# A sparse attention layer: ring of 17 in place of 20 gather slots, and a later write of the flag for the branch

## The chip, the cores and the metric

The kernel runs on one core of a Trainium2 chip. The metric is the device time of one execution in microseconds. Before the change, five runs gave a median of 1885.34 us, between 1882.17 and 1888.16 us. One more execution was taken with the hardware profiler; all durations come from it.

The engines have short names in the profile: PE (TensorE, matmuls and transposes), PEld (its weight loads), DVE (VectorE), ACT (ScalarE), POOL (GpSimd) and SP (SyncE). Each works through its own queue in order.

## The reference

One graph layer over 4096 nodes with 512 features, 8 heads of 64, and a 4096 x 4096 adjacency matrix of 0 and 1 with some 17 edges in a row:

```python
hs, ht = layer_norm(x), layer_norm(h_target)             # ln1
q = (ht @ Wq + bq) / 8;  k = hs @ Wk + bk;  v = hs @ Wv + bv
logits = where(edge_mask != 0, q @ k.T, -1e30)           # for each head
ctx = softmax(logits) @ v
ht = layer_norm(ht + ctx @ Wo + bo)                      # ln2
x = layernorm(x + ht + gelu(ht @ W1) @ W2)               # W1: 512 x 2048
```

## The kernel before

The kernel uses that the matrix is sparse. It has two programs in one: a fast path for inputs like these, and `general_path`, a dense version that a branch at the end runs only when the fast path has found that its assumptions fail (a row with too many neighbours, a mask that is not all ones, sums out of range). The branch reads one number, `flag`.

**Lists (to about 650 us).** For each tile of 128 rows of the matrix, four quarters of 1024 columns are loaded. ACT takes the sign of a quarter (L727), DVE multiplies it by the column's number and takes the eight largest of each segment (L734). The numbers of a row's neighbours end in a record of that row. `sort` ranks the rows of one half of the matrix by their number of neighbours (`PARTS`: the first part is rows 0 to 2047, the second 2048 to 4095), and scatters the records in that order to DRAM (L852). So a tile of 128 targets later has a fixed capacity, from 39 down to 11 neighbours (`CAPS_A`, `CAPS_B`). Meanwhile PE projects all nodes to keys and values and writes them as rows of 4 KB to DRAM, `kvd`.

**Attention (about 305 to 1770 us).** A tile's neighbours are taken in groups of up to three (`S`, list `SG`: 211 groups, 603 gathers). For each neighbour POOL issues one indirect DMA (L962, called from `issue`) that brings 128 rows of 4 KB, 512 KB, into one slot of the `ring`. Per group DVE multiplies the keys by the query (L1189), sums per head (L1193), ACT takes the exponential (L1197, L1207; a third neighbour's values are scaled on ACT, L1170 and L1173), DVE multiplies the values by it (L1153) and, in the second part, adds the second neighbour's values to the first's (L1157). PE transposes the slots into one PSUM sum (L1161). A slot is free when L1161, or for the second neighbour of the second part L1157, has read it. `finish` divides, applies `Wo` (L1074 to L1088) and the second layer norm; its power on POOL is L686. The query of a tile comes from `front`: a gather of target rows, a scale on ACT (L988), transposes (L992) and `Wq` (L1001, L1003).

**Feed-forward (about 330 to 1866 us).** Pairs of tiles (`GROUPS`, 17 of them, the first and last single) go through W1, GELU (L1297, L1300) and W2 (L1306) in `feed`. `end` adds, normalises (L1253 to L1270; power again L686) and scatters the rows to the output by an indirect DMA (L1274).

**What sets the order.** The stages are Python generators that yield a cost; `_weave` always continues the one that is furthest behind, so attention, feed-forward and list work are interleaved as the program is written. The framework then places the instructions in the engines' queues by its own estimate of the times, and adds the waits. In the attention stage each pair of tiles has the same cost (`UNIT`), whatever its number of neighbours.

**The ring.** It has 20 slots of 4 KB a partition. While the first part is processed, groups use slots 0 to 16. Slots 17 and 18 (`wide`) and 19 (`tools`) are the work space of the lists of the second part: quarters of the matrix, their signs, and the small tiles of `sort`. From group 106 on, the first whose tile belongs to the second part by its place (`i >= NA`), groups use all 20 slots. `request(k)`, called when the values of the group before k have been handed on (line after `values` in `attention`), issues the gathers of all groups up to k + 4 in the first part and k + 5 in the second (`AHEAD` is 4).

**The verdict and the branch.** `verdict` collects what was found wrong into one number in PSUM (L1242), and DVE writes `flag` from it (L1243). It stands at the end of `attention`. After all work, `values_load` (L1421) makes each of the five engines load `flag` into a register, and `tc.If` (L1422) is a branch on each of them.

Of the kernel before, what the change touches and what calls it, by code (L numbers as in the profile page):

```python
# [17 lines left out]
P = 128  # L18
# [349 lines left out]
U8 = mybir.dt.uint8  # L368
# [75 lines left out]
def adj_resnorm_kernel(  # L444
# [58 lines left out]
    S = 3  # L503


    RING = (17, 20)

# [8 lines left out]

    flag = const.tile([1, 1], I32, name="flag")

    def row_bcast(pool, v, name):
# [12 lines left out]
    with tc.tile_pool(name="keep", bufs=1) as keep:  # L532
# [17 lines left out]
        with ExitStack() as late:  # L550
# [13 lines left out]

            ring = kp.tile([P, RING[1], 2 * D], F32, name="kv")
            wide = [ring[:, 17 + i, :].bitcast(I32) for i in range(2)]
            tools = ring[:, 19, :]
            signs = [tools[:, i * QW // 4:(i + 1) * QW // 4].bitcast(U8) for i in range(3)]
            dec_w = tools[:, 768:768 + SEG * 8].bitcast(U16).rearrange("p (b s e) -> p b s e",
                                                                       b=2, s=SEG)  # L570
            turns = {"wide": 0, "signs": 0}

            def turn_of(name, places):
                turns[name] += 1
                return places[turns[name] % len(places)]

# [31 lines left out]
            def list_constants():  # L608
                io = turn_of("wide", wide)
# [4 lines left out]
                io = turn_of("wide", wide)  # L614
# [92 lines left out]
            def quarter(i, h):  # L707
                if i < NA + FILL:
                    a = ring[:, (i * NQ + h) % DEEP, :].bitcast(I32)
                else:  # L710
                    a = turn_of("wide", wide)
                nc.sync.dma_start(a, adj[i * P:(i + 1) * P, h * QW:(h + 1) * QW])
                return a

            def edges(i):
# [4 lines left out]
                for h in range(NQ):  # L720
# [4 lines left out]

                    sg = turn_of("signs", signs)
                    nc.scalar.activation(sg, a, AF.Sign, accum_out=dpart[:, i, h:h + 1])  # L727
# [11 lines left out]
                    yield 2.0  # L739
                dec = dec_w  # L740
                nc.vector.tensor_single_scalar(dec[:, 0], cand, 255, op=ALU.bitwise_and)
# [64 lines left out]
            def sort(part):  # L806
# [5 lines left out]
                nc.vector.tensor_copy(R[:, :, DEG], deg[:, me])  # L812
                dif, rank = tools[:, 928:928 + n], tools[:, 944:944 + n]
                ranki, b16 = tools[:, 960:960 + n].bitcast(I32), tools[:, 976:984].bitcast(BF16)
# [3 lines left out]
                nc.vector.tensor_scalar(dif, deg[:, me], 0.0, float(NB - 1), op0=ALU.max,  # L818
                                        op1=ALU.min)
                nc.vector.tensor_scalar(b16, dif, -1.0, float(NB - 1), op0=ALU.mult, op1=ALU.add)  # L820
                if part:
                    oh = turn_of("wide", wide).bitcast(BF16)
                else:
                    oh = wp.tile([P, NB * n], BF16, name="oh")
# [3 lines left out]
                ohf = oh.rearrange("p b i -> p (b i)")  # L828
                pos = turn_of("wide", wide).bitcast(F32)
                pos = pos[:, :NB * n].rearrange("p (b i) -> p b i", b=NB)  # L830
# [11 lines left out]
                for c in range(2):  # L842
# [3 lines left out]
                    nc.vector.tensor_add(posf[:, sl], pa, posf[:, sl])  # L846
                nc.vector.tensor_mul(pos, pos, oh)
                nc.vector.tensor_reduce(rank, pos.rearrange("p b i -> p i b"), AX.X, ALU.add)
                nc.vector.tensor_copy(ranki, rank)
                yield 10.0  # L850
# [160 lines left out]
            place = [0]  # L1011
            for i, _, n in SG:
                if place[-1] + n > RING[i >= NA]:
                    place[-1] = 0
                place.append(place[-1] + n)
            first_b = next(k for k, (i, _, _) in enumerate(SG) if i >= NA)
            issued = [0]

# [4 lines left out]

            def request(k):


                ahead = AHEAD + (1 if k >= first_b else 0)
                while issued[0] <= min(k + ahead, len(SG) - 1):
                    issue(issued[0])
                    mine = set(range(place[issued[0]], place[issued[0]] + SG[issued[0]][2]))  # L1030
                    for m in range(k, issued[0]):
                        assert not mine & set(range(place[m], place[m] + SG[m][2]))
                    issued[0] += 1

            def issue(k):

                i, j0, n = SG[k]
                if j0 == 0:
# [97 lines left out]
            def attention():  # L1136
# [37 lines left out]

                request(0)
                yield 0.0
                k = 0
                for group in GROUPS:
# [3 lines left out]
                    for i in group:  # L1182
                        cps = ps.tile([P, KC, P], F32, name="cps", bufs=2)
                        while k < len(SG) and SG[k][0] == i:
# [15 lines left out]
                            if pend:  # L1200
                                values(*pend.pop())
                                request(k)
                            advance()
# [17 lines left out]
            def verdict():  # L1221
# [20 lines left out]
                nc.tensor.matmul(pb, b1, ones_bf[:, 0:1], start=True, stop=True)  # L1242
                nc.vector.tensor_scalar(flag, pb, 0.5, None, op0=ALU.is_gt)  # L1243

# [37 lines left out]
            def feed(g):  # L1282
# [88 lines left out]
            def prepare():  # L1371
# [10 lines left out]
                nm = turn_of("wide", wide)  # L1382
                nc.sync.dma_start(nm[:NT, :P], nodemask.rearrange("(c p) -> c p", p=P))
# [71 lines left out]
```

## Time and profile before

| what | value |
|---|---|
| median of five runs | 1885.34 us |
| profiled execution, its own time | 1887.54 us |
| its span, first to last instruction | 1885.5 us |
| PE busy | 1701.6 us, 7030 matmuls |
| DVE busy | 1429.2 us |
| ACT busy | 1233.3 us |
| POOL busy | 885.0 us |
| gathers (L962, kv) | 603, 1136 ns each on POOL |
| last matmul ends | 1866.8 us |
| granted PE clock, mean | 0.957 |

The page gives busy time by engine, then the costliest groups of instructions by line, then waits. A line such as `DVE a L10 <- PE b L20: 5.0, 3, 2.1` in the view of waits says that VectorE stood idle before the instructions of line 10 that write a, for 5.0 us in 3 waits, the longest 2.1 us, until PE's instruction of line 20 released it. "issue" in place of a releaser is idle time for which the profile shows no wait. The table by stages has for each stretch of time its length, and then each engine's busy time with its number of instructions, the granted PE clock, the DMA engines' busy share and GB/s. A row of one line's instructions gives their number, minimum, median and maximum duration in ns, and the first and last start.

### The profile page before, as it was taken

The numbers are of one execution on the slowest core, as the hardware profiler recorded it, in microseconds if no ns is written. First come the engines' busy times: TensorE is split into PE (matmuls) and PEld (weight loads), VectorE is DVE, ScalarE is ACT, GpSimd is POOL, SyncE is SP. The second block draws the span as 40 slices with busy tenths as digits, with TensorE's granted clock in tenths as the row PEclk, the third lists the DMA queues.
The fourth block names the chain that finished last, engine by engine and source line by source line (L and its number), as shares of the span: only waits on it lengthen the run. The fifth ranks groups of instructions, "written<-read, shape, count | busy, mean of one in ns | idle before, by whom it ended". The sixth has DMA issues, their size and how long they took to land. (4 is left out here: it accounts for less than half of the span.)

```text
span 1885.5 us, 22906 instructions
## 1 busy us (share of the span) xinstructions
PE 1701.6 (90%) x7030; PEld 1101.8 (58%) x7030; DVE 1429.2 (76%) x2595; ACT 1233.3 (65%) x3127; POOL 885.0 (47%) x804
## 2 busy tenths in 40 slices
PE   7989883698998989999989989999989899999996
PEld 3444331565665656676666666666656565666664
DVE  6999855999998747777868889888777778778200
ACT  5777634586886747776777777876757567677311
POOL 1000144644545565657576676665646554644101
PEclk9999987798999989999999999999999999999998
DMA  9999949878876656868688788777756666765000
GB/s 352 372 371 372 354 155 351 315 273 299 315 276 227 206 179 217 279 216 294 232 283 293 259 283 299 273 238 236 245 194 215 230 224 216 244 215 180 23 1 24
DMA packets 147757, 463.28 MB, mean 246 GB/s; under 512 B 24468, under 2 KB 29160, under 8 KB 147624
## 3 DMA queue, kind: packets, MB, share of 16 engines
q0 software_dynamic: 95696, 342.19, 53.2%
q1 hardware_dynamic: 44112, 96.44, 14.3%
q10 hardware_dynamic: 7816, 23.08, 3.2%
q8 instruction: 58, 0.95, 0.2%
q14 instruction: 75, 0.61, 0.1%
HBM read 430.76 MB, written 30.89 MB: 245 GB/s over the span
## 5 line engine op out<-in xcount | busy, mean ns | idle before, releaser
L962 POOL DMA_INDIRECT kv<-kvd,rec x603 | 685.1, 1136 | 484.9 <-PE cps L1161 214.8
L1297 PE MATMUL pf<-h2T,w 128*128 128x256 f32 (+1 forms) x2176 | 481.0, 373 | 5.6 <-issue 2.8
L1306 PE MATMUL po<-w,gt 128*128 128x512 f32 x1024 | 464.3, 594 | 0.0
L1297 PEld LDWEIGHTS pf<-h2T,w 128*128 128x128 f32 x2176 | 393.8, 194 | 68.3 <-issue 20.0
L1189 DVE TENSOR_TENSOR kv<-kv,tq 128x1536 f32<-128x1536 f32 (+2 forms) x211 | 352.4, 1676 | 106.7 <-DMA kv<-kvd,rec 83.3
L1173 ACT ACTIVATE kv<-kv,pa 128x64 f32<-128x64 f32 x1520 | 391.6, 336 | 3.8
L1193 DVE TENSOR_REDUCE lg<-kv 128x24 f32<-128x1536 f32 (+2 forms) x211 | 350.5, 1667 | 1.5 <-ACT pa L1170 0.3
L1161 PE MATMUL cps<-ident,kv 128*128 128x128 f32 x2008 | 266.8, 281 | 45.9 <-DMA kv<-kvd,rec 23.7
L1161 PEld LDWEIGHTS cps<-ident,kv 128*128 128x128 f32 x2008 | 240.1, 145 | 116.5 <-issue 89.2
L1306 PEld LDWEIGHTS po<-w,gt 128*128 128x128 f32 x1024 | 186.3, 191 | 188.5 <-issue 188.0
L1153 DVE TENSOR_TENSOR kv<-kv,p 128x1024 f32<-128x1024 f32 (+1 forms) x211 | 249.6, 1189 | 50.9 <-ACT p L1197 40.9
L686 POOL TENSOR_TENSOR n_rs<-n_ve,mhalf 128x2 f32<-128x2 f32 (+2 forms) x51 | 45.2, 887 | 343.7 <-DVE n_ve L679 171.2
L727 ACT ACTIVATE kv<-kv 128x1024 uint8<-128x1024 int32 x128 | 134.9, 1055 | 84.8 <-DMA kv<-in_adj_dram 46.7
L927 PE MATMUL pq<-wk,h2T 128*128 128x512 f32 x256 | 125.8, 636 | 15.9 <-ACT h2T L912 9.4
L1300 ACT ACT_TABLE_LOAD x107 | 137.3, 1283 | 1.6
L734 DVE MAX8 cand<-kv 128x8 uint16<-128x103 uint16 (+1 forms) x640 | 132.1, 252 | 0.5
L1300 ACT ACTIVATE gt<-pf 128x512 f32<-128x512 f32 x128 | 76.4, 597 | 85.0 <-PE pf L1297 72.3
L1001 PE MATMUL t<-wq,tq 128*128 128x512 f32 x256 | 117.5, 601 | 13.7 <-ACT tq L995 9.8
L1088 PE MATMUL t<-wo,rb 128*128 128x512 f32 x256 | 119.7, 612 | 1.7 <-DVE rb L1078 1.7
L927 PE MATMUL pq<-wv,h2T 128*128 128x512 f32 x256 | 115.5, 593 | 0.4 <-ACT tq L929 0.4
L1197 ACT ACTIVATE p<-lg 128x24 f32<-128x24 f32 (+2 forms) x179 | 33.6, 188 | 107.2 <-DVE lg L1193 77.8
L927 PEld LDWEIGHTS pq<-wk,h2T 128*128 128x128 f32 x256 | 50.7, 205 | 83.2 <-issue 60.4
(155 smaller groups left out, 1561.5 us busy)
## 6 DMA issues: line engine op xcount, KB each, us to landing
kv<-in_adj_dram SPq DMA_DIRECT2D x128, 512.0 KB
kvd<-tq ACTq DMA_DIRECT2D x24, 512.0 KB
kv<-kvd,rec POOLq DMA_INDIRECT x603
kv<-in_L_gnn_h_target_dram SPq DMA_DIRECT2D x32, 256.0 KB
kv<-in_x_dram SPq DMA_DIRECT2D x15, 512.0 KB
rest_d<-gid SPq DMA_DIRECT2D x32, 160.0 KB
w<-in_L_gnn_W_dram SPq DMA_DIRECT2D x4, 1024.0 KB
kvd<-kv ACTq DMA_DIRECT2D x8, 512.0 KB
```

The costliest lines, as they stand in the source:

```text
L727: nc.scalar.activation(sg, a, AF.Sign, accum_out=dpart[:, i, h:h + 1])
L734: nc.vector.max(cand[:, h * SQ + s, :], wd[:, w0:w1])
L927: nc.tensor.matmul(pkv, hT[:, kc, j * P:(j + 1) * P], w[:, kc, :], start=kc == 0, stop=kc == KC - 1)
L962: nc.gpsimd.indirect_dma_start(out=dst, out_offset=None, in_=table[:, :], in_offset=bass.IndirectOffsetOnAxis(ap=idx, axis=0))
L1153: nc.vector.tensor_tensor(v4, v4, p[:, j0:j0 + m, :].unsqueeze(3) .to_broadcast([P, m, H, HD]), ALU.mult)
L1161: nc.tensor.matmul(cps[:, c, :], kv[:, j, D + c * P:D + (c + 1) * P], ident, is_transpose=True, start=j0 + j == 0 and c == 0, stop=j0 + n ...
L1173: nc.scalar.mul(v, v, pa[:, hd:hd + 1])
L1189: nc.vector.tensor_tensor(kv[:, :n, :D], kv[:, :n, :D], tq[:, :D].unsqueeze(1).to_broadcast([P, n, D]), ALU.mult)
L1193: nc.vector.tensor_reduce(lg[:, :n, :], kv[:, :n, :D].rearrange("p j (h d) -> p j h d", h=H), AX.X, ALU.add)
L1297: nc.tensor.matmul(pf[:, k, :], w1[(f0 + k) // KC][:, kc, (f0 + k) % KC * P:((f0 + k) % KC + 1) * P], h2T[:, kc, :w], start=kc == 0, stop= ...
L1300: nc.scalar.activation(gt, pf, AF.Gelu_apprx_tanh)
L1306: nc.tensor.matmul(po[j], gt[:, k, j * P:(j + 1) * P], w2[(f0 + k) // KC][:, (f0 + k) % KC, :], start=False, stop=f0 + k == FC - 1, skip_g ...
```

## The change

The change takes the ring back to one depth and one distance of requests, gives the lists' work space tiles of its own, and puts one instruction between the verdict and the flag.

- `RING` is 17 for both parts. `wide`, `tools`, `signs` and `turn_of` go; quarters, signs, and the tiles of `sort` and of the list's decoding are tiles of the pool `lp` with the same sizes and numbers of buffers.
- `request` goes. `attention` first issues groups 0 to 4, and then `issue(k + AHEAD)` for each group, in both parts. `issue` itself is the same.
- `verdict` writes `raised`. In `feed`, after the last `end` has been emptied, DVE computes `flag` as the maximum of `raised` and `raised`, with one element of the last result row, `xs[-1]`, as a scalar operand that is bypassed. So this instruction waits for the last activation (L1270), and each engine's load of `flag` waits for this instruction.

```diff
-    RING = (17, 20)
+    RING = 17
...
     flag = const.tile([1, 1], I32, name="flag")
+    raised = const.tile([1, 1], F32, name="raised")
...
-            ring = kp.tile([P, RING[1], 2 * D], F32, name="kv")
-            wide = [ring[:, 17 + i, :].bitcast(I32) for i in range(2)]
-            tools = ring[:, 19, :]
-            signs = [tools[:, i * QW // 4:(i + 1) * QW // 4].bitcast(U8) for i in range(3)]
...
+            ring = kp.tile([P, RING, 2 * D], F32, name="kv")
...
                 else:
-                    a = turn_of("wide", wide)
+                    a = lp.tile([P, QW], I32, name="a", bufs=2)
                 nc.sync.dma_start(a, adj[i * P:(i + 1) * P, h * QW:(h + 1) * QW])
...
-                    sg = turn_of("signs", signs)
+                    sg = lp.tile([P, QW], U8, name="sg", bufs=3)
...
-            for i, _, n in SG:
-                if place[-1] + n > RING[i >= NA]:
+            for _, _, n in SG:
+                if place[-1] + n > RING:
                     place[-1] = 0
                 place.append(place[-1] + n)
-            first_b = next(k for k, (i, _, _) in enumerate(SG) if i >= NA)
-            issued = [0]
...
-            def request(k):
-                ahead = AHEAD + (1 if k >= first_b else 0)
-                while issued[0] <= min(k + ahead, len(SG) - 1):
-                    issue(issued[0])
...
-                    issued[0] += 1
...
-                request(0)
+                for k in range(AHEAD + 1):
+                    issue(k)
...
                                 values(*pend.pop())
-                                request(k)
+                                issue(k + AHEAD)
...
-                nc.vector.tensor_scalar(flag, pb, 0.5, None, op0=ALU.is_gt)
+                nc.vector.tensor_scalar(raised, pb, 0.5, None, op0=ALU.is_gt)
...
                     while ends:
                         wind_up()
+                    nc.vector.scalar_tensor_tensor(flag, raised, xs[-1][0:1, 0:1], raised,
+                                                   op0=ALU.bypass, op1=ALU.max)
```

More of the change, by code (lines that the diff above doesn't have):

```diff
@@ L561, in adj_resnorm_kernel @@
             psi = mid.enter_context(tc.tile_pool(name="psi", bufs=1, space=PSUM))
-            ring = kp.tile([P, RING[1], 2 * D], F32, name="kv")
-            wide = [ring[:, 17 + i, :].bitcast(I32) for i in range(2)]
-            tools = ring[:, 19, :]
-            signs = [tools[:, i * QW // 4:(i + 1) * QW // 4].bitcast(U8) for i in range(3)]
[L569 to L575, printed above, removed]
+            ring = kp.tile([P, RING, 2 * D], F32, name="kv")
             def xrows(n):
@@ L608, in list_constants @@
             def list_constants():
-                io = turn_of("wide", wide)
+                io = lp.tile([P, QW], I32, name="a", bufs=2)
                 nc.gpsimd.iota(io[:, :SQ * WS], pattern=[[0, SQ], [2, WS]], base=1,
@@ L613, in list_constants @@
                 nc.vector.tensor_copy(lio, io[:, :WQ])
-                io = turn_of("wide", wide)
+                io = lp.tile([P, QW], I32, name="a", bufs=2)
                 nc.gpsimd.iota(io[:, :2 * SEG], pattern=[[1, 2], [QW, NQ], [2 * WS, SQ]], base=0,
@@ L739, in edges @@
                     yield 2.0
-                dec = dec_w
+                dec = lp.tile([P, 2, SEG, 8], U16, name="dec")
                 nc.vector.tensor_single_scalar(dec[:, 0], cand, 255, op=ALU.bitwise_and)
@@ L812, in sort @@
                 nc.vector.tensor_copy(R[:, :, DEG], deg[:, me])
-                dif, rank = tools[:, 928:928 + n], tools[:, 944:944 + n]
-                ranki, b16 = tools[:, 960:960 + n].bitcast(I32), tools[:, 976:984].bitcast(BF16)
+                dif = pool.tile([P, n], F32, name="dif")
                 nc.vector.scalar_tensor_tensor(dif, deg[:, me], float(RE), cnt[:, me], op0=ALU.min,
@@ L819, in sort @@
                                         op1=ALU.min)
+                b16 = pool.tile([P, n], BF16, name="b16")
                 nc.vector.tensor_scalar(b16, dif, -1.0, float(NB - 1), op0=ALU.mult, op1=ALU.add)
                 if part:
-                    oh = turn_of("wide", wide).bitcast(BF16)
+                    oh = pool.tile([P, QW], I32, name="a", bufs=2).bitcast(BF16)
                 else:
@@ L828, in sort @@
                 ohf = oh.rearrange("p b i -> p (b i)")
-                pos = turn_of("wide", wide).bitcast(F32)
+                pos = pool.tile([P, QW], I32, name="a", bufs=2).bitcast(F32)
                 pos = pos[:, :NB * n].rearrange("p (b i) -> p b i", b=NB)
@@ L847, in sort @@
                 nc.vector.tensor_mul(pos, pos, oh)
+                rank = pool.tile([P, n], F32, name="rank")
                 nc.vector.tensor_reduce(rank, pos.rearrange("p b i -> p i b"), AX.X, ALU.add)
+                ranki = pool.tile([P, n], I32, name="ranki")
                 nc.vector.tensor_copy(ranki, rank)
@@ L1022, in step @@
                     del gens[i]
-            def request(k):
-                ahead = AHEAD + (1 if k >= first_b else 0)
-                while issued[0] <= min(k + ahead, len(SG) - 1):
-                    issue(issued[0])
-                    mine = set(range(place[issued[0]], place[issued[0]] + SG[issued[0]][2]))
-                    for m in range(k, issued[0]):
-                        assert not mine & set(range(place[m], place[m] + SG[m][2]))
-                    issued[0] += 1
             def issue(k):
+                if k >= len(SG):
+                    return
                 i, j0, n = SG[k]
@@ L1381, in prepare @@
                     nc.vector.tensor_copy(Rf[:, :, RST + 1], nm[:, i0:i0 + n])
-                nm = turn_of("wide", wide)
+                nm = lp.tile([P, QW], I32, name="a", bufs=2)
                 nc.sync.dma_start(nm[:NT, :P], nodemask.rearrange("(c p) -> c p", p=P))
```

## The prediction

> **What bounds the kernel now.** I read the page's busy shares first, then the busy time by stage, then the waits of VectorE and GpSimd in each stage, then the instructions at the branch.
>
> ```profile
> span 1885.5 us, 22906 instructions
> PE   1701.6 (90%) x7030; PEld 1101.8 (58%) x7030; DVE 1429.2 (76%) x2595; ACT 1233.3 (65%) x3127; POOL 885.0 (47%) x804
> ```
>
> TensorE (PE) is busy 90% of the span and takes its work in one fixed order, so the time is PE's work plus PE's idle time. What matters is which late result leaves PE idle. The stages below are cut at 1024 us, where the requests for the second part begin, at 1250 us, where the second part's first two pairs of tiles are done, and at 1740 us, where the last gathered rows are used.
>
> ```profile
> core 0: us, PE busy (x) PEld busy (x) DVE busy (x) ACT busy (x) POOL busy (x), PEclk, DMA share, GB/s
> 700.00:1024.00 324.00, 312.13 (x1476) 218.01 (x1475) 251.62 (x253) 236.67 (x645) 197.02 (x177) 1.00 0.76 257
> 1024.00:1250.00 226.00, 211.49 (x922) 143.28 (x921) 207.41 (x215) 175.17 (x486) 150.76 (x131) 0.98 0.80 277
> 1250.00:1740.00 490.00, 458.60 (x1918) 305.37 (x1916) 377.12 (x401) 336.58 (x883) 265.44 (x232) 0.98 0.66 222
> 1740.00:1871.00 131.00, 126.80 (x540) 84.67 (x537) 20.30 (x82) 31.02 (x65) 10.32 (x13) 1.00 0.05 15
> ```
>
> The first row is the first part's attention, which already runs with a ring of 17 and requests four groups ahead: PE is idle 11.9 of 324 us (3.7%). The next two rows run with 20 slots and five groups ahead: PE is idle 14.5 of 226 us and 31.4 of 490 us (6.4% each). In the row from 1024 us VectorE (DVE) is busy 207.4 of 226 us (92%): this is the one stage where DVE has little room. From 1740 us PE does feed-forward alone.
>
> Waits of DVE in the three attention stages, one line from 700 to 1024 us, two from 1024 to 1250 us and one from 1250 to 1740 us:
>
> ```profile
> DVE kv L1189 <- DMA kv<-kvd,rec: 29.0, 15, 5.2
> ...
> DVE kv L1153 <- ACT p L1197: 6.6, 9, 2.3
> DVE kv L1189 <- issue: 4.8, 2, 2.6
> ...
> DVE kv L1189 <- DMA kv<-kvd,rec: 24.3, 12, 6.8
> ```
>
> L1189 is the first use of a gathered group. With four groups ahead it waits 29.0 us in 324 us for the gathers; with five ahead it waits for none in the stage from 1024 us. What GpSimd (POOL) waits for between 1024 and 1760 us, before it issues gathers:
>
> ```profile
> POOL kv L962 <- DVE kv L1157: 74.0, 36, 6.1
> POOL kv L962 <- PE cps L1161: 68.7, 35, 5.9
> ```
>
> L1157 and L1161 are the last readers of a slot. So the gathers are issued when a slot comes free: the ring's depth sets the lead.
>
> **The change part by part.** *The lists' work space* goes from three ring slots (12 KB a partition) to tiles of the same sizes and counts. In the order of the two programs every engine has the same instructions up to the first request of the second part, so nothing moves before about 1020 us: 0 us. The buffers' counts and turns are the same, and so are the waits that they set.
>
> *The ring and the requests.* In the second part each group is requested one group later. I took from the trace, for each group, the first issue, the landing (last semaphore event of its DMAs) and the use (L1189). From 700 to 1024 us (four ahead): 52 groups, one each 6.2 us, landing on average 4.5 us before use. From 1024 to 1250 us: 38 groups, one each 5.9 us, 8.2 us before use. From 1250 to 1740 us: 69 groups, one each 7.1 us, 11.6 us before use. One group later leaves 8.2 - 5.9 = 2.3 us and 11.6 - 7.1 = 4.5 us on average. The mean hides the late ones, so I compared each group's use with the landing of the *next* group, which is when it would land itself. From 1024 to 1250 us the next lands after the use in 10 of 38 groups, by 17.1 us in sum; from 1250 to 1740 us in 12 of 69, by 21.6 us. Delays carry over, since a late use frees its slot late: with use delay d(k) = max(d(k-1), d(k-5) + lateness(k)) and nothing absorbed, d is 10.1 us at 1250 us and 26.4 us at the end.
>
> What reaches PE: in the stage from 1024 us DVE has 18.6 us free, of which 13.8 us are waits for others in which a late group costs nothing. Bounds 0 and 17.1 us; I take 8 us, near the 10.1 us of the recursion, since DVE is 92% busy there and PE's transposes (L1161) wait for DVE. From 1250 to 1740 us the bounds are 0 and 26.4 - 10.1 = 16.3 us; I take 0, since the nearest row, 700 to 1024 us, has 29.0 us of such waits in a shorter time with PE less idle than here: with DVE 77% busy, PE's feed-forward covers them. That cover is gone where DVE has no room, which is the 8 us above.
>
> In the orders of instructions ScalarE (ACT) loads its tables six times more after the change. At 1.28 us (L1300, 137.3 us by 107) that is 7.7 us on an engine that is busy 69% from 1250 us: 0 us taken, 7.7 us at most. On POOL, n_rs (L686), the row gathers for xt and tq, and the output scatters each stand one group of gathers earlier relative to the kv gathers; that could gain, and is a rival below.
>
> A rule of the Trainium skill speaks against a cost here. "DMA: Bandwidth & Descriptors", section "Anatomy of one DMA", gives a DMA from GpSimd as 2.0 us plus its bytes at 436 GB/s, so an estimate by that page is 3.2 us for a 512 KB gather. The trace has 9.6 us from a group's first issue to its landing (three gathers, other traffic beside), so the trace decides; by the page the lateness above would be nearly nil and the sum below would be 0.3 us.
>
> *The flag.* The verdict's last instruction (L1243) now writes `raised`; one more 1x1 DVE instruction after the last ACT result (L1270, ends 1870.63 us) writes `flag`. All five engines load it before the branch:
>
> ```profile
> L1243 DVE TENSOR_SCALAR flag<-t x1: 145/145/145, 1809.8 to 1809.8; 1x1 int32<-1x1 f32 x1
> L1421 SPq TENSOR_LOAD <-flag x1: 472/472/472, 1810.0 to 1810.0; - x1
> L1421 PEldq TENSOR_LOAD <-flag x1: 487/487/487, 1860.7 to 1860.7; - x1
> L1421 DVEq TENSOR_LOAD <-flag x1: 542/542/542, 1869.6 to 1869.6; - x1
> L1421 ACTq TENSOR_LOAD <-flag x1: 463/463/463, 1869.8 to 1869.8; - x1
> L1421 POOLq TENSOR_LOAD <-flag x1: 508/508/508, 1870.7 to 1870.7; - x1
> ```
>
> SP's load moves by 61 us and PE's by 10 us, but nothing is queued behind them except the end of the program, which waits for POOL. POOL's load stands behind the last scatter, which is not held up: it still waits for L1270 alone.
>
> ```profile
> L1422 POOLq EVENT_SEMAPHORE  x5: 17/43/43, 1873.9 to 1874.2; - x5
> ...
> L1422 POOLq COMPARE_BRANCH  x1: 53/53/53, 1871.2 to 1871.2; - x1
> ...
> L1422 POOLq INC_SWDGE_SEM  x1: 2175/2175/2175, 1874.3 to 1874.3; - x1
> ```
>
> After the branch POOL takes 2.6 us to its next instruction, then 2.2 us for INC_SWDGE_SEM and 8.2 us for a drain (1876.5 to 1884.7), then the end. The new instruction takes about 0.15 us (L1243's 145 ns) and a semaphore to POOL about 0.15 us (L1262's end at 1868.81 to L686 at 1868.97): POOL's load starts near 1870.95 instead of 1870.67, so the tail grows by 0.3 us. The longest branch is PE's (3.34 us); late, it ends near 1875 us, far before POOL's drain, so it costs nothing. Five engines fetching at once is not in the trace: at least 0.1 us in all, at most POOL's 2.6 us doubled, so 2.9 us.
>
> "Advanced Engine Details and Errata", section "Control Flow Timing", gives a compare-and-branch about 108 ns, while "Runtime: NRT & Kernel Launch", section "Instruction fetch mechanics", says a taken branch out of the window waits for a fetch by DMA. The 2.6 us gap agrees with the second; by the first the flag's tail term would still be 0.3 us.
>
> The sum: 8 + 0 + 0 + 0.3 = 8.3 us. The profiled execution took 1887.54 us, 2.04 us beyond its span, and lies 2.2 us above the median of 1885.34 us, inside the runs' 1882.17 to 1888.16. On the median: 1893.6, rounded 1893.5 us.
>
> **The rivals.** *The lead was spare* (chance 0.23): PE's idle time in the second part is named by other chains (L992 and L1114 behind ACT), and 700 to 1024 us shows PE better filled with the short lead. Then only the tail's 0.3 us is left: 1885.6 us, within 0.2%. Against it: DVE's 92%.
>
> *Delays add up to the end* (0.16): each late group from 1250 us on also reaches PE, since L1161 and the next group's slot wait for it: 26.4 + 0.3 gives 1912 us, from 1901 us up. Against it: 23% of DVE's time is free there.
>
> *Faster* (0.11): POOL is one queue in order; a kv gather that waits for a slot holds n_rs and the row gathers behind it, and they feed PE's waits for ACT in the second part (L992 for h 7.8 us, L1114 for h 4.8 us). With one group fewer ahead they come earlier; all of it gone is 12.6 us (1873 us), half is 6.3: 1879 us. It decides if those two waits fall by more than DVE's waits for gathers cost PE. Against it: DVE's waits for n_rs are 9.4 us in all.
>
> That the flag does what it says is nearly free either way: four of five loads already stand behind the last work, so this part decides nothing.
>
> **How the numbers follow.** The forecast (4 to 15 us more: 1889 to 1900 us) has 0.50, the rivals 0.23, 0.16 and 0.11. About 0.2% (3.8 us) is what a measurement of this kernel can tell from no change: faster 0.11, same 0.23, slower 0.50 + 0.16 = 0.66. The range reaches from 1883, which leaves out the faster rival, to 1906 us, which takes the first half of the delays that add up and leaves out some 0.08.
>
> **What would show it.** Right: from 1024 to 1250 us DVE waits 10 to 20 us for gathers (none now) and PE's idle time there rises by about 8 us, with the end of attention (1740 us) later by as much; from 1250 us DVE waits more for gathers and PE's idle share stays near 6.4%; flag loads on all engines start together some 0.3 us after the last L1270, and the span's tail after PE's last matmul (18.7 us) grows by under 1 us. Wrong: PE's idle time changes mainly at waits for ACT (another order in the queues), or gathers land as far ahead of use as now.

## The result and the profile after

The changed kernel takes 1877.92 us (median of 30 runs, 1874.62 to 1885.11) beside 1885.19 us (56 runs, 1876.35 to 1893.77) for the kernel before on the same chips. The ratio is 0.9968, with a 95% interval of 0.9958 to 0.9977: the change makes the kernel 0.3% faster. The prediction said 1893.5 us, slower. The profiled execution after has a span of 1875.2 us. Lines are renumbered: L1189 is now L1170, L1161 L1141, L1157 L1137, L992 L983, L1001 L992, L1074 L1054, L1084 L1064, L1114 L1094, L995 L986, L1076 L1056, L1092 L1072, L1105 L1085, L1118 L1098, L962 L953, L988 L979, L1270 L1251, L1421 L1405 and L1422 L1406.

The page's first lines, of the kernel after:

```profile
span 1875.2 us, 22927 instructions
PE 1695.2 (90%) x7030; PEld 1094.7 (58%) x7030; DVE 1430.4 (76%) x2596; ACT 1242.1 (66%) x3133; POOL 887.7 (47%) x804
```

PE is busy 90% of the span as before. The table by stages, with each engine's busy time, the clock, the DMA share and GB/s:

```profile
700.00:1024.00 324.00, 313.54 (x1476) 218.51 (x1475) 250.49 (x252) 235.41 (x640) 196.81 (x174) 0.99 0.74 251
1024.00:1250.00 226.00, 204.49 (x892) 138.44 (x891) 195.19 (x200) 163.59 (x459) 144.30 (x124) 0.96 0.77 262
1250.00:1740.00 490.00, 470.66 (x1989) 313.15 (x1988) 392.83 (x418) 357.82 (x922) 274.74 (x241) 0.99 0.70 231
```

Two stages went opposite ways. From 1024 to 1250 us PE is busy 7.0 us less than before (211.49) in the same time, from 1250 to 1740 us 12.1 us more (458.60). The first is what the prediction feared: DVE now waits for gathers, and PE for DVE. DVE's waits in that stage, after:

```profile
DVE kv L1170 <- DMA kv<-kvd,rec: 18.4, 7, 7.4
```

and PE's:

```profile
PE cps L1141 <- DVE kv L1137: 19.2, 5, 6.4
```

Before, DVE had none of the first kind there, and PE 5.6 us of the second:

```profile
PE cps L1161 <- DVE kv L1157: 5.6, 2, 4.2
```

The gain is in the stage from 1250 us. Over both stages PE is idle 5.1 us less. The two profiled spans differ by 10.3 us, more than the medians; PE's busy time itself fell by 6.4 us for the same 7030 matmuls (1701.6 and 1695.2 us), at a mean granted clock of 0.957 and 0.963. PE's waits in the stage from 1250 us, before:

```profile
PE t L992 <- ACT h L1092: 7.8, 2, 5.0
PE t L1084 <- issue: 7.3, 1, 7.3
PE t L1084 <- ACT tq L995: 3.8, 1, 3.8
```

and after, where none is over 3.2 us:

```profile
PE t L992 <- ACT tq L986: 5.4, 3, 2.5
PE t L1094 <- ACT h2T L1098: 3.6, 2, 3.2
PE t L983 <- ACT h L1072: 2.6, 2, 2.3
```

All of before's long waits there are at the PSUM buffer `t`. There is one such buffer, and the front of a tile (F, the transposes L992, and Q, Wq, L1001) and the finish of another (R, the transposes of the reciprocals, L1074; A and W, L1084 and L1088; H, L1114) take turns in it. The longest gap, in the timeline before, with lines of other work left out:

```profile
1473.26 0.60 PE L992 MATMUL t<-ident,tq 128*128 128x128 f32 x4
...
1474.30 1.28 ACT L1197 ACT_TABLE_LOAD   x1 [1.83 <-DVE lg L1193]
...
1478.05 1.22 DVE L1189 TENSOR_TENSOR kv<-kv,tq 128x1024 f32<-128x1024 f32 x1 [1.01 <-DMA kv<-kvd,rec]
...
1481.04 0.19 ACT L1197 ACTIVATE p<-lg 128x16 f32<-128x16 f32 x1 [3.08 <-DVE lg L1193]
1481.25 1.28 ACT L1300 ACT_TABLE_LOAD   x1
...
1482.54 0.60 ACT L1300 ACTIVATE gt<-pf 128x512 f32<-128x512 f32 x1
...
1483.03 1.50 ACT L995 ACTIVATE tq<-t,b1r,cols 128x128 f32<-128x128 f32 x4
...
1484.59 1.11 PE L1084 MATMUL t<-ident,tq 128*128 128x128 f32 x4 [7.28 <-issue]
```

The front's transposes (F) are in `t` at 1473.9 us. ACT should empty them, but L995 stands in ACT's queue behind an exponential (L1197), which waits for DVE, which waits for a gather, and behind a GELU (L1300) with its table load. L995 starts at 1483.03 us, 9.2 us after the transposes. In these 9.2 us ACT is idle for 3.5 us (3.08 of them before that exponential; the gather itself holds DVE for 1.01 us), loads tables for 2.6 us and does its other work in the rest: the late gather is the smaller part, the place in ACT's queue the larger. The finish's A, next in `t` and next on PE, starts 0.06 us after L995 ends, after 7.28 us of idle time. The profile calls it "issue"; the times of L995 and A show what it was.

### The profile page after: what moved, and what is told of

Its sections match the earlier page's. It is cut to its first block, busy times and chain, and to the rows that moved or that the text cites. A ratio compares the mean times of both kernels' runs of the same rounds, so it can differ in the third digit from the quotient of the medians.

```text
span 1875.2 us, 22927 instructions
## 1 busy us (share of the span) xinstructions
PE 1695.2 (90%) x7030; PEld 1094.7 (58%) x7030; DVE 1430.4 (76%) x2596; ACT 1242.1 (66%) x3133; POOL 887.7 (47%) x804
## 5 line engine op out<-in xcount | busy, mean ns | idle before, releaser
L953 POOL DMA_INDIRECT kv<-kvd,rec x603 | 692.4, 1148 | 498.4 <-PE cps L1141 226.9
L1278 PE MATMUL pf<-h2T,w 128*128 128x256 f32 (+1 forms) x2176 | 473.8, 369 | 3.8 <-issue 1.9
L1287 PE MATMUL po<-w,gt 128*128 128x512 f32 x1024 | 470.9, 601 | 0.4 <-issue 0.4
L1170 DVE TENSOR_TENSOR kv<-kv,tq 128x1536 f32<-128x1536 f32 (+2 forms) x211 | 352.3, 1676 | 115.2 <-DMA kv<-kvd,rec 103.6
L1278 PEld LDWEIGHTS pf<-h2T,w 128*128 128x128 f32 x2176 | 389.2, 192 | 68.3 <-issue 22.6
L1141 PE MATMUL cps<-ident,kv 128*128 128x128 f32 x2008 | 266.8, 280 | 61.9 <-DMA kv<-kvd,rec 22.6
L1141 PEld LDWEIGHTS cps<-ident,kv 128*128 128x128 f32 x2008 | 238.8, 145 | 136.6 <-issue 87.4
L992 PE MATMUL t<-wq,tq 128*128 128x512 f32 x256 | 119.8, 611 | 15.5 <-ACT tq L986 11.4
L723 DVE MAX8 cand<-sg 128x8 uint16<-128x103 uint16 (+1 forms) x640 | 132.1, 252 | 0.5
L716 ACT ACTIVATE sg<-kv 128x1024 uint8<-128x1024 int32 x84 | 88.7, 1057 | 56.5 <-DMA kv<-in_adj_dram 23.5
```

The lines of the kernel that those rows point to most:

```text
L723: nc.vector.max(cand[:, h * SQ + s, :], wd[:, w0:w1])
L953: nc.gpsimd.indirect_dma_start(out=dst, out_offset=None, in_=table[:, :], in_offset=bass.IndirectOffsetOnAxis(ap=idx, axis=0))
L992: nc.tensor.matmul(pq, hT[:, kc, :], wq[:, kc, :], start=kc == 0, stop=kc == KC - 1)
L1141: nc.tensor.matmul(cps[:, c, :], kv[:, j, D + c * P:D + (c + 1) * P], ident, is_transpose=True, start=j0 + j == 0 and c == 0, stop=j0 + n ...
L1170: nc.vector.tensor_tensor(kv[:, :n, :D], kv[:, :n, :D], tq[:, :D].unsqueeze(1).to_broadcast([P, n, D]), ALU.mult)
L1278: nc.tensor.matmul(pf[:, k, :], w1[(f0 + k) // KC][:, kc, (f0 + k) % KC * P:((f0 + k) % KC + 1) * P], h2T[:, kc, :w], start=kc == 0, stop= ...
```

## The experiments

All ratios are to the kernel before, run beside each experiment on the same chip (medians there: 1882.28 us for the first four experiments, 1886.16 for the next four, 1879.89 for the four after them and 1884.05 for the last four), with 95% intervals. The ratios are not the quotients of two medians; they differ from them by up to 0.2%.

**The flag alone**: the kernel before with `raised` and the late instruction of the change (its last two hunks) and nothing else.

> The kernel before with the flag written late, and nothing else: every engine keeps the order of instructions of the kernel before. Theory A (the gain of the change comes with the second part's requests and the order of instructions that they bring): the time stays or grows by the tail's 1.6 us (18.7 us from PE's last matmul to the end before, 20.3 us after), so 1885 to 1888 us. Theory B (the late flag itself gains, because no engine takes its branch and fetches code while others still compute): 1878 us, as the whole change.

Measured: 1879.85 us, ratio 0.9986 [0.9972, 0.9999]: no cost that can be measured. In the profile the tail from PE's last matmul to the end is 20.4 us.

**All but the flag**: the changed kernel, with the flag written by the verdict.

```diff
-                nc.vector.tensor_scalar(raised, pb, 0.5, None, op0=ALU.is_gt)
+                nc.vector.tensor_scalar(flag, pb, 0.5, None, op0=ALU.is_gt)
```

> The changed kernel with the verdict writing the flag directly, as before: same order of instructions as the changed kernel on every engine. Theory A: 1876 to 1877 us, the changed kernel's 1877.9 us less 1.6 us of tail. Theory B: 1885 us.

Measured: 1875.26 us, 0.9964 [0.9948, 0.9981], tail 18.8 us. The gain is not the flag's.

**20 slots, four groups ahead**: the kernel before, one number changed.

```diff
-                ahead = AHEAD + (1 if k >= first_b else 0)
+                ahead = AHEAD
```

> The kernel before with 20 slots in the second part, but requests four groups ahead as in the first. It takes the distance of the requests alone, with slots to spare. Theory A in the form that later requests clear the way on GpSimd's queue for the row gathers and powers: 1877 us or less. Theory C (the gain is in the order that the framework happened to choose for ring and distance together): anywhere between 1875 and 1890 us, unrelated to the changed kernel's time. If the depth of 17 itself matters: 1885 us.

Measured: 1857.14 us, 0.9864 [0.9843, 0.9886]. So the later request is what gains, and the 20 slots, which the change gives up, are worth some 18 us more.

**17 slots, four ahead, work space still in the ring's tile**:

```diff
-    RING = (17, 20)
+    RING = (17, 17)
...
-            ring = kp.tile([P, RING[1], 2 * D], F32, name="kv")
+            ring = kp.tile([P, 20, 2 * D], F32, name="kv")
...
-                ahead = AHEAD + (1 if k >= first_b else 0)
+                ahead = AHEAD
```

> The changed kernel's ring of 17 and requests four ahead, flag written early, but the work space of the lists still in three ring slots, as before. Same order of instructions as the changed kernel. If the work space costs nothing, as predicted: equal to the kernel of the changed ring with the early flag within 1 us, 1876 to 1877 us. Theory D (the tiles of their own are the gain): 1885 us.

Measured: 1874.55 us, 0.9959 [0.9943, 0.9976], as without the late flag above. The work space's own tiles are worth nothing.

**A request taken apart.** `issue` does two things: it issues gathers of keys and values, and with a tile's first group it begins the front of that tile (and prefetches a record). These two kernels give each its own distance in the second part:

```diff
+            begun = [0]
...
             def request(k):
...
+                extra = 1 if k >= first_b else 0
+                for done, ahead, work in ((begun, AHEAD + 0 * extra, begin),
+                                          (issued, AHEAD + 1 * extra, issue)):
+                    while done[0] <= min(k + ahead, len(SG) - 1):
+                        work(done[0])
+                        done[0] += 1
...
```

Here `begin` has the lines of `issue` that stand under `if j0 == 0`. Gathers five ahead, fronts four:

> The kernel before with the two things that a request does taken apart: in the second part the gathers of keys and values are issued five groups ahead as before, but a tile's front (the gather of its target rows, its scale, transposes and Wq) and its list are begun four groups ahead. In the built programs this has nearly the order of the kernel with 20 slots and four groups ahead (10 of POOL's and 15 of PE's instructions placed otherwise), and not that of the kernel before. Theory F (what costs 25 us at five ahead is that the fronts, and with them the order of everything, come a group earlier; the distance of the gathers is undone by the framework's placing): 1857 us, between 1853 and 1862. Theory G (the gathers' own distance costs it, since slots are claimed a group earlier): 1882 us, between 1876 and 1888.

Measured: 1858.92 us, 0.9851 [0.9820, 0.9883]. Gathers four ahead, fronts five (0 and 1 exchanged):

> The other half: gathers of keys and values four groups ahead, fronts and lists five groups ahead, 20 slots in the second part. Its order is nearly that of the kernel before (11 of POOL's and 15 of PE's instructions placed otherwise). Theory F (fronts): 1882 us, between 1877 and 1888. Theory G (gathers): 1857 us, between 1853 and 1863.

Measured: 1886.29 us, 0.9995 [0.9976, 1.0013]. The number that asks for the gathers four or five groups ahead is worth nothing here; the whole gain goes with that of the fronts. This does not say what a real change of the gathers' distance is worth, since the number hardly moved them. The framework places the gathers by its own estimate: between the two kernels with fronts four ahead only 10 of POOL's 804 instructions stand elsewhere in the built programs, against 196 between the kernel before and the one with 20 slots and four ahead. In the traces of the two, a group's first gather is issued on average 30.5 us (four) and 30.1 us (five) before its use from 1250 to 1700 us. PE's waits in the stage from 1250 us in this second kernel are those of the kernel before (L1085 is L1084 there):

```profile
PE t L1085 <- ACT tq L995: 11.6, 2, 7.7
PE t L992 <- ACT h L1093: 8.1, 2, 5.3
PE t L1075 <- ACT tq L995: 4.4, 2, 3.8
```

and in the first kernel (gathers five, fronts four) little is left of them:

```profile
PE t L1085 <- ACT tq L995: 1.8, 3, 0.8
PE t L1089 <- DVE rb L1079: 1.7, 1, 1.7
```

The same steps as in the gap above, in the timeline of that first kernel (gathers five, fronts four): the finish has A and W done before the front's F takes `t`, and L995 comes 2 us after it.

```profile
1454.23 0.60 PE L1075 MATMUL t<-ident,rb 128*128 128x128 f32 x4
...
1462.43 0.60 PE L1085 MATMUL t<-ident,tq 128*128 128x128 f32 x4
1462.87 3.60 PE L1089 MATMUL t<-wo,rb 128*128 128x512 f32 x8
...
1470.97 0.66 PE L992 MATMUL t<-ident,tq 128*128 128x128 f32 x4 [0.20 <-issue]
...
1473.67 1.49 ACT L995 ACTIVATE tq<-t,b1r,cols 128x128 f32<-128x128 f32 x4
```

**Three ahead.** `ahead = AHEAD - (1 if k >= first_b else 0)`, for fronts and gathers together, with 17 and with 20 slots:

> 17 slots in both parts, four groups ahead in the first part and three in the second; otherwise the kernel before. Beside the kernel with 17 slots and four ahead (1874.6 us). Theory S (slots that are spare beside the groups in flight give the time: 17 slots with four groups in flight leave 5, as 20 with five do, against 2): 1857 us, between 1850 and 1864. Theory L (the lead itself gives it: DVE waits longer for gathers with a group fewer ahead): 1885 us, over 1879. Theory F (fronts a group earlier only spoil the order, so another group later is no worse): 1874 us, between 1868 and 1878.

> 20 slots in the second part and three groups ahead there; otherwise the kernel before. Beside 20 slots and four ahead (1857.1 us). Theory S (spare slots, 8 here): 1850 us, under 1855. Theory L (lead): 1868 us, over 1862. Theory F (the order with the fronts later, depth of 20 unchanged): 1857 us, between 1852 and 1862.

Measured: 1869.79 us, 0.9905 [0.9878, 0.9932], and 1862.96 us, 0.9867 [0.9835, 0.9900]. The kernel before ran 3.9 us slower beside these four than beside the first four, so the ratios count. With 20 slots three ahead is as good as four (0.9864), as theory F has it, and the 8 spare slots of theory S bring nothing. With 17 slots three ahead is better than four (0.9959, the intervals lie apart), so theory L fails, but by the ratio it gains more than theory F said (in microseconds it lies inside F's range). Taken by the ratios, no one of the three holds for both.

**17 slots with the fronts five ahead**: gathers four, fronts five, `RING = (17, 17)`. If the change is two things that add, this is its cost alone.

> 17 slots in both parts and gathers of keys and values four groups ahead, as after the change, but in the second part fronts and lists are begun five groups ahead, as before it; flag as before. If the change is two things that add (17 slots in place of 20 cost some 17 us, fronts a group later gain some 25 us), only the cost is left here: 1875 + 25 = 1900 us, between 1892 and 1908. If the fronts' distance matters only together with 20 slots, 1875 us, between 1870 and 1880.

Measured: 1903.60 us, 1.0113 [1.0086, 1.0140]. They add. The four corners, with the changed kernel as the last:

| | fronts five ahead | fronts four ahead |
|---|---|---|
| 20 slots | 1 (before) | 0.9864 |
| 17 slots | 1.0113 | 0.9968 (after) |

Down a column, 17 slots cost 1.13% or 1.04%, some 21 or 20 us; along a row, the fronts a group later gain 1.36% or 1.45%, some 26 or 27 us. 21 - 27 = -6 us is what the change does. The stage from 1250 us of this kernel, and of the one with 20 slots and four ahead:

```profile
1250.00:1740.00 490.00, 450.35 (x1857) 297.29 (x1856) 374.00 (x399) 335.26 (x871) 263.49 (x231) 0.97 0.66 219
```

```profile
1250.00:1740.00 490.00, 480.24 (x2040) 320.38 (x2039) 389.06 (x454) 351.62 (x915) 256.30 (x230) 1.00 0.66 219
```

In it PE is idle 39.7 and 9.8 us of 490, with before (31.4) and after (19.3) between them. These two kernels differ in slots and in fronts. To see the slots alone, compare along the same distance of the fronts. With fronts five ahead, DVE waits for gathers there for 24.3 us with 20 slots (before) and 65.0 us with 17:

```profile
DVE kv L1190 <- DMA kv<-kvd,rec: 65.0, 25, 7.0
```

With fronts four ahead it waits 9.8 us with 20 slots and 22.3 us with 17 (after):

```profile
DVE kv L1189 <- DMA kv<-kvd,rec: 9.8, 3, 7.5
```

```profile
DVE kv L1170 <- DMA kv<-kvd,rec: 22.3, 13, 4.0
```

So both moves change these waits, the slots and the fronts. Nor is it idle time alone that differs: PE is busy for 1710.1 us in the first kernel (granted clock 0.956) and 1691.2 us in the second (0.966), for the same 7030 matmuls. What moved the clock was not tested.

**Which step of the front.** Fronts of the second part with a step held back or brought forward. First, five ahead, with one more step between the row gather and the rest:

```diff
                 gather(t, h_target, rec[:, TGT:TGT + 1])
                 yield
+                if i >= NA:
+                    yield
```

> The kernel before, with everything requested five groups ahead in the second part, but a front of the second part waits one more step after its row gather is issued, so that its scale, transposes and Wq come a step later; only the row gather and the list stay a group early. Theory F1 (it is the distance of the fronts' work on ACT and PE): 1857 us, between 1853 and 1862. Theory F2 (it is the early row gather and list): 1884 us, over 1877. Theory T (it is the order in which front and finish take turns in the one PSUM buffer t; the program has the order of the kernel before up to about the middle of the last stage, with the front's transposes three times between H of the one tile and R of the next, and the order of the changed kernel from there): between the two, 1863 to 1876.

Measured: 1869.79 us, 0.9936 [0.9913, 0.9959]. Next, four ahead, without the step between row gather and scale:

```diff
                 gather(t, h_target, rec[:, TGT:TGT + 1])
-                yield
+                if i < NA:
+                    yield
```

> 20 slots and everything requested four groups ahead (1857 us), but a front of the second part does its scale in the same step as its row gather, so that scale, transposes and Wq come a step earlier; only the row gather and the list stay where they are. Theory F1 (the distance of the fronts' work on ACT and PE): 1884 us, over 1877. Theory F2 (the row gather and the list): 1857 us, between 1853 and 1862. Theory T (the turns in the PSUM buffer t, which are here those of the run with the held front in all but one place): the same as that run within 6 us, and between 1863 and 1876.

Measured: 1873.25 us, 0.9954 [0.9936, 0.9973]. Last, five ahead, Wq alone a step later (the added `yield` stands ahead of `pq`):

> The kernel before, with everything requested five groups ahead in the second part, but the front's Wq of the second part waits one more step; the row gather, the scale and the transposes stay a group early. If the early transposes, which take the PSUM buffer t between R and A or between H and R, are what costs, this stays near the kernel before: over 1875 us. If it is the early Wq, 1857 us, between 1853 and 1864.

Measured: 1865.61 us, 0.9907 [0.9878, 0.9936]. The first two came out as the turns in `t` said, between the ends and 3.5 us apart. Where in the stage the time goes can be seen too. From the traces I took PE's idle time between the first L1189 of one pair of tiles and of the next, and the turns that PE took in `t`, by the start of their instructions:

| kernel | tiles 21 to 24: turns, idle us | 25 and 26 | 27 to 30 |
|---|---|---|---|
| before | HFRQA, 13.2 | RFA, 8.6 | RFA and RFQA, 9.6 |
| front held, five ahead | HFRQA, 13.9 | RAW, RFA, 9.3 | RAW, RFA, 1.3 |
| front early, four ahead | HFRQA, 11.4 | RAW, RFA, 9.0 | RAW, RFA, 1.3 |
| Wq held, five ahead | HFRQA, 11.4 | RFA, 7.2 | RFA, 3.5 |
| 20 slots, four ahead | HRFQA, 5.6 | RAW, RFA, 0.7 | RAW, RFA, 3.5 |
| after | HRFQA, 6.2 | RAW, RFA, 5.5 | RAW, RFA, 5.7 |

In tiles 21 to 24 the loss goes with the turns: 11 to 14 us where F comes between one tile's H and the next one's R, 6 us where it does not. In tiles 27 to 30 the two kernels with a front held or early have the turns of the changed kernel and lose 1.3 us. But the changed kernel itself loses 5.7 us there and the one with 20 slots 3.5 us, and in tiles 25 and 26 all four have the same turns and lose between 0.7 and 9.3 us. So the turns alone do not tell all. The run with Wq held fits neither of its forecasts: the early transposes do not keep it near before.

**A PSUM buffer for the fronts.** Do the turns cost because there is one buffer? To keep the number of PSUM buffers as it is, the exponentials `p` move to SBUF and the masked ones are written over them, and the fronts get the buffer:

```diff
-                pt = ps.tile([P, KC, P], F32, name="t")
+                pt = ps.tile([P, KC, P], F32, name="tf")
...
-                pq = ps.tile([P, D], F32, name="t")
+                pq = ps.tile([P, D], F32, name="tf")
...
-                pm = sp.tile([P, MAXE, H], F32, name="pm", bufs=1)
+                pm = p
...
-                                p = ps.tile([P, MAXE, H], F32, name="p")
+                                p = sp.tile([P, MAXE, H], F32, name="p", bufs=1)
...
```

> The kernel before (20 slots and everything five groups ahead in the second part), with a PSUM buffer of its own for the fronts' transposes and Wq. Its bank comes from the exponentials p, which move to SBUF, and the masked exponentials are written over p. The turns of front and finish on PE are those of the kernel before, and the control with p in SBUF alone is run beside it. Theory T (a front that takes the one PSUM buffer between two steps of a finish makes the finish wait for its evacuation on ACT): the waits are gone, at least 12 us under its control, and within 8 us of the same kernel at four ahead. Theory Q (it is the order of the queues of PE and ACT, whatever the buffer): within 5 us of its control, and over 18 us above the same kernel at four ahead.

> The same with 20 slots and everything four groups ahead in the second part. Theory T: little is left to gain here, 0 to 8 us under its control, and within 8 us of the five-ahead kernel with the fronts' own buffer. Theory Q: as its control, and over 18 us under the five-ahead kernel.

The controls have the last two changes without the first two:

> Control: the kernel before with the exponentials p in SBUF and the masked ones written over them, and the one PSUM buffer shared as before. Both theories: near the kernel before, within 8 us, and some 25 us above the same control at four ahead; what p's place costs or gains by itself is in both controls.

> Control: the same with everything four groups ahead. Both theories: near the kernel with 20 slots and four ahead (ratio 0.986 to the kernel before), within 8 us, and some 25 us under the control at five ahead.

| all requests | own buffer | control |
|---|---|---|
| five ahead | 1885.97 us, 1.0007 [0.9991, 1.0024] | 1897.81 us, 1.0063 [1.0044, 1.0082] |
| four ahead | 1868.49 us, 0.9921 [0.9898, 0.9944] | 1875.41 us, 0.9954 [0.9937, 0.9972] |

Both theories miss. A buffer of their own gains 0.56% (some 11 us) at five ahead and 0.33% at four, and the distance between five and four shrinks only from 1.09% to 0.86%. The waits of A and R for L995 are gone at five ahead, but this one has come in their place: Wq waits for the same L995.

```profile
PE tf L1001 <- ACT tq L995: 13.1, 4, 4.8
```

So a buffer for each takes away at most a smaller part of what five ahead costs (0.23% of 1.09%, less than the intervals resolve). What is left must lie elsewhere. The waits point to the order of ACT's queue, in which the front's evacuation comes late whoever waits for it, but no run here shows that, and which place in the queue costs what stays open. Moving `p` to SBUF cost 0.6% and 0.9%, more than the 8 us that the controls' forecasts allowed.

## Why the prediction was wrong, point by point

**The step that failed** is the first sentence on the requests: "In the second part each group is requested one group later." The text then priced the gathers of keys and values alone. The same call begins the tile's front, with a row gather, a scale, transposes, Wq and their evacuations on ACT. That half, with the tile's list and record, moves the order of all queues (between the kernel before and the one with 20 slots and four ahead 196 of POOL's and 750 of PE's instructions stand elsewhere in the built programs) and gains 26 to 27 us; it had no term in the sum. The other half, which was priced, moves almost nothing: with fronts four ahead, the number for the gathers moves 10 of POOL's instructions and 15 of PE's, and the time is the same (0.9864 and 0.9851, intervals overlapping). What shortens the lead of the gathers is the ring's depth. That the gain comes with the fronts is shown; by which of the moved instructions it comes is open, as said above.

**The table of landings was wrong as well.** It took POOL's gathers in the order of the groups. In the built program 439 of 603 are not in that order. With each gather matched to its group by its slot, before's gathers land on average 2.4, 6.8 and 4.8 us before use in the three stages (up to 1700 us in the last), not 4.5, 8.2 and 11.6. After they land 2.4, 3.2 and 3.7 us before. Put through the prediction's own recursion, these landings before would give 29.6 us of delay at 1250 us and 120.7 us at the end, far over the 20 or 21 us that 17 slots cost. So the recursion is no measure of the cost, and that its 26.4 us came near is luck. The prediction also took PE's work as fixed; in these profiles it is 1691 to 1710 us for the same matmuls.

**The ring: right mechanism, too small.** In the stage from 1024 us the forecast was 8 us: PE's idle time rose from 14.5 to 21.5 us there, and DVE's waits for gathers from none to 18.4 us, as foretold. At the 140th group the changed kernel is 16 us behind (its L1189 starts at 1253.1 in place of 1237.0 us); at the last group it is 4 us ahead (1734.2 and 1738.4 us), which the prediction had the other way round. But the light stage, taken at 0 because "with DVE 77% busy, PE's feed-forward covers them", was not covered: 17 slots take PE's idle time there from 31.4 to 39.7 us with fronts five ahead and from 9.8 to 19.3 us with fronts four ahead. The whole cost is 20 or 21 us, inside the bounds of 0 to 33.4 and nearer to "Delays add up to the end" than to the forecast. Why: a slot's lead was spent. By slot, the gathers land 4.8 us before use with 20 slots and 2.2 us with 17 (fronts five ahead), 9.8 and 3.7 us with fronts four ahead, from 1250 to 1700 us, and DVE's waits for them grow with it (24.3 to 65.0 us and 9.8 to 22.3 us). How the waits reach PE is argued from the gap above: an exponential that waits for DVE holds up the evacuations behind it on ACT.

**Lists' work space: 0 us**, right (17 slots with the work space in the ring's tile or in tiles of its own: 0.9959 and 0.9964). **ACT's six table loads: 0 us**: nothing here contradicts it, no run took them alone.

**The flag: 0.3 us of the tail, measured 1.6.** All five loads start together at 1859.0 us, as forecast, 0.28 us after L1251's end. POOL's load, its semaphores after the branch, and the branch:

```profile
L1405 POOLq TENSOR_LOAD <-flag x1: 516/516/516, 1859.0 to 1859.0; - x1
...
L1406 POOLq EVENT_SEMAPHORE  x5: 17/43/43, 1863.5 to 1863.9; - x5
...
L1406 POOLq COMPARE_BRANCH  x1: 53/53/53, 1859.6 to 1859.6; - x1
```

The term that was too small is the way from the branch to POOL's next instruction: 3.9 us, against 2.6 us before. It was 3.4 us in the kernel with the late flag alone and 2.7 us in the changed kernel with the early one, and 2.5 to 2.8 us in every other kernel here; so it goes with the five branches at one time. "Runtime: NRT & Kernel Launch", section "Instruction fetch mechanics", has a taken branch out of the window wait for a fetch by DMA. These gaps agree with such a wait, and that five fetches slow each other is argued, not shown. In the time of the whole kernel the 1.6 us are lost in the runs' scatter.

**The faster rival** had the right side, with a cause that the traces bear out only in part. Both of its waits fell: L992 behind ACT's h from 7.8 to 2.6 us in the stage from 1250 us, L1114 behind h from 4.8 to 2.0 us in the stage before, together 8.0 of its 12.6 us. But L992 waits there for L1092, which copies the finish's result out of `t`, a step with no power and no new row gather ahead of it, and the longest waits before, those of L1084 (7.3 and 3.8 us), were not on its list. Nor did the row gathers come earlier for those who wait for them: from 1250 to 1760 us, ACT's waits for them rose from 10.7 to 17.5 us.

```profile
ACT tq L988 <- DMA tq<-in_L_gnn_h_target_dram,rec: 10.7, 4, 5.4
```

```profile
ACT tq L979 <- DMA tq<-in_L_gnn_h_target_dram,rec: 17.5, 6, 6.7
```

DVE's waits for the powers did fall, from 9.4 to 2.0 us between 1024 and 1760 us. No run took this part alone. That its 1879 us for half of the waits lies near the measured 1877.92 is luck: the measured time is the sum of two effects of 20 us and more, and the rival priced neither.

**What beats both** is to keep the 20 slots and take only the fronts' distance from the change: 1857.14 us, 0.9864.

## What to carry to other kernels

When a distance of prefetch is changed, list everything that the call issues and price each part: here the number for the transfers, which gave it its name, moved almost none of them, and the compute that rode along was worth 1.4%. Look in the built program whether a distance of prefetch is still there at all. Before lead times are read from a trace, match transfers to their users by buffer and not by their place in the queue. A change that moves the time by 0.3% can be two effects of over 1% each; undoing its parts one at a time, all corners of the table, shows it, and shows the version that keeps only the gain.

## What was not expected of the hardware

Five engines that take a branch at the same time each come later to their next instruction: POOL 3.9 us after its branch (3.4 us in a second kernel) against 2.5 to 2.8 us in the sixteen kernels where the other engines had branched before it. SP needs 3.8 and 3.7 us against 2.4 to 2.7, DVE 4.0 and 3.6 against 2.8 to 3.1, ACT 3.5 and 3.8 against 2.4 to 3.0.
